# One shared pool of buffers, a throw-away tile for row sums, a plan that follows its ranks, and layer 1's diagonal addition on GpSimd

## The chip, the cores and the metric

The kernel runs on one core of a Trainium2 chip. A core has a matrix engine (TensorE, PE in the profile; its weight loads are shown apart as PEld), a vector engine (VectorE, DVE), a scalar engine (ScalarE, ACT), a general engine (GpSimd, POOL) and SyncE (SP), whose queue only issues transfers here. Each engine works through its own instructions in program order, and waits at a semaphore where an instruction needs something that isn't there yet. All matrices are 32-bit floats. The metric is the device time of one launch in microseconds (us); less is better.

## What is computed

Sixteen independent graphs ("batches") of N = 1024 nodes with 128 features each, and a 1024 x 1024 matrix `adj` for each, pass four layers. Each layer starts with a layer norm and a ReLU and ends with an addition to x:

```python
# layer 0, three times over, h the normed input (no relu after the third)
h = h @ W + b
nh = h / max(norm(h), EPS);  cos = nh @ nh.T
h = relu((adj * cos) @ h)
# layer 1 (y is 0 where nodemask is off)
y = relu(((1 + eps) * h + adj.T @ h) @ W1 + b1) @ W2 + b2
# layer 2
h = h @ W;  attn = softmax(where(adj > 0, tanh(s1[:, None] + s2[None, :]), -1e15))
y = where(rows without a neighbour, input, attn @ h)
# layer 3
h = x @ W.T + b;  e = h A h.T + its transpose
att = softmax(where(adj > 0, e, 0), axis=1) * adj
hp = relu(att @ h)          # then three sigmoid gates over [x, hp]
```

## The kernel before

**Tiles.** A node block is 128 nodes, so a graph has 8 blocks (`NB`), and a 1024 x 1024 matrix is 8 pieces of 128 x 1024. Products are made in halves of 512 columns, one PSUM bank each. `adj` is read twice: transposed (`adjT`, function `turn`, for layers 0, 2 and 3), and as it stands (`adjL`, function `layer1`). For `adjT` the transfer puts squares of 32 x 32 in place (L1518) and DVE turns each square (L1526). For batch 0 the pieces come as they are (`raw`, L1494) and PE turns them.

**Layer 0 and layer 3** need a symmetric product (`Square`, from L1341). `row(j, s)` makes only the blocks on and over the diagonal on PE (L1363). The blocks under it are mirrored: PE transposes them (L1373) from copies that `keep` made in the tile `above` of 22 blocks, or, in the batches 1 to 13, the lower left quarter goes through HBM: DVE transposes 32 x 32 squares into `above` (L1385), SP's queue stores them (L1412) and fetches them into `got` (L1422). DVE then multiplies each half with `adjT` (L1598 in layer 0, L1863 and L1904 in layer 3), and PE adds the products up (L1431, L1442).

**Row sums.** Layer 2 needs to know which rows have no neighbour. ACT copies each piece of `adjT` onto itself and keeps the sum of each row in `su` (L1529), so all who use `adjT` come after that copy.

**Layer 1.** For each of the 8 pieces `adjL` a transfer is issued (L1476, `load_adj`); then DVE adds (1 + eps) on the diagonal of the piece, one 128 x 128 block (`ident_e`, L1643); then PE multiplies (L1431). 

**GpSimd's work**: the inverse square roots of the layer norms (`rstd`) and of layer 0's norms (`rn`), both at L1165; one product of layer 3's end (`z`, L2008); four products in the last two batches (L1900); and at the start the transfers of the parameters (L278).

**The order of the work.** Nothing is issued as it is written down. Every operation becomes an `Op` with an engine, a cost in us, what it reads and writes, and a rank: a due time from the table `TIMES` plus the batch number times `PERIOD` (L1070). `Plan.order` (L135) then builds one list; each engine's program is its part of that list. It keeps a clock for each engine. At each step it looks at all operations whose predecessors are in the list, works out the earliest time at which each could start (its engine is free, its inputs are there, its buffer is free), takes the engine with the earliest of those, and on it, among the operations that can start within `WINDOW` = 0.05 us of that time, the one of lowest rank. An operation of a batch more than `AHEAD` = 2 past the oldest unfinished one isn't taken, transfers excepted. Operations marked `port` (those of DVE that read two tiles of SBUF, and some others) and all of GpSimd's share one more clock in the plan, `port`, so that the plan never lays one over the other:

```python
if o.port and port > at:
    at = port
```

**Buffers.** A `Buf` takes a slot in a pool when its first writer is placed, and gives it back after its last user. `POOLS` says how many slots each pool has, `KINDS` which pool a kind uses, how many of it there may be in all, and how many by batches other than the oldest. Before the change there are separate pools: 16 slots for `adjT`, 5 for `adjL` and `raw`, 3 for x, 13 (`big`) for all other tiles of 128 x 1024 and a little more (`w4`, `chunk`), and 2 for `above`.

Of the kernel before, what the change touches and what calls it, by code (L numbers as in the profile page):

```python
# [34 lines left out]
class Buf:  # L35


    def __init__(self, kind, shape, name):
        self.kind, self.shape, self.name = kind, shape, name
        self.slot = self.t = None  # L40
        self.uses = 0
        self.seen, self.users = [], []
        self.end = 0.0
# [12 lines left out]
class Plan:  # L56
# [78 lines left out]
    def order(self):  # L135
# [12 lines left out]
        rows = {e: i for i, e in enumerate(self.LATENCY)}  # L148
        while ready:
# [4 lines left out]
            found = []  # L154
            for o in ready:
                if o.batch > oldest + self.ahead and o.engine != "DMA":
                    continue
                at = max(free[o.engine], o.from_)
                if o.port and port > at:
                    at = port  # L160
                if o.new:
                    need, room = {}, {}
                    for b in o.new:
                        need[b.kind] = need.get(b.kind, 0) + 1
                    for k, n in need.items():
                        pool, most, share = self.kinds[k]
                        if total[k] + n > most or (o.batch > oldest and young[k] + n > share):
                            at = None
                            break
                        room[pool] = room.get(pool, 0) + n  # L170
                    if at is not None:
                        for pool, n in room.items():
                            if len(state[pool]) < n:
                                at = None
                                break
                            at = max(at, state[pool][n - 1][0])
                    if at is None:
                        continue
                found.append((at, o))
            if not found:  # L180
                stuck = [b.name for o in ready if o.batch == oldest for b in o.new]
                raise RuntimeError(f"no slot for any of {stuck}")
            first = min(found, key=lambda f: (f[0], rows[f[1].engine]))
            at, o = min(
                (f for f in found if f[1].engine == first[1].engine and f[0] <= first[0] + self.window),
                key=lambda f: f[1].rank,
            )
# [34 lines left out]
def tile_adj_preln(  # L222
# [40 lines left out]
    FLAGS = set("CabcdkxhyzTGmrHWMD3n")  # L263
# [4 lines left out]
    nc.vector.memset(half, 0.5)  # L268
    mhalf = const.tile([P, NB], F32, name="mhalf")
# [55 lines left out]
    for load_it in first:  # L325
# [11 lines left out]
    POOLS = {"adjT": 16, "adjL": 5, "x": 3, "big": 13, "above": 2, "got": 1, "bank": 8, "small": 29, "row": 6, "hbm": 3, "hrow": 2, "mask": 5, "dot": 12}  # L337
    KINDS = {
        "adjT": ("adjT", 16, 16), "adjL": ("adjL", 5, 5), "x": ("x", 3, 3), "w4": ("big", 9, 5),
        "chunk": ("big", 10, 12), "above": ("above", 2, 1), "got": ("got", 1, 1), "ps": ("bank", 7, 8),  # L340
        "acc": ("bank", 7, 8), "small": ("small", 7, 16), "row": ("row", 3, 3), "hbm": ("hbm", 3, 3),
        "hrow": ("hrow", 1, 1), "mask": ("mask", 5, 5), "dot": ("dot", 6, 11),
    }
    PERIOD, AHEAD, WINDOW = 145.06, 2, 0.05

    TIMES = {
        "T DMA raw <0": [51.6, -92.65, -42.9, 3.5, 39.85, 7.55, 4, 14.6],
        "T PE raw <0": [8.95, 14, 0.9, 0.1, 1.8, 11.5, 24.3, 8.7, 10.25, 24.85, 23.15, 30.8, 27.8, 31.75,
            37.1, 39.05],
        "T ACT adjT <0": [10.4, 39.05, 8.5, 13.4, 18.8, 14.95, 18.55, 20.55, 23.6, 34, 35.15, 28.45, 39.25,  # L350
            43.8, 44.95, 62.3],
        "T DVE su <0": [53.8],
        "x DMA x <0": [51.55, -93.7],
        "0 DVE st <0": [3.5, 4.1],
        "0 DVE mv <0": [9.55],
        "0 POOL rstd <0": [4.05],
        "0 DVE nb <0": [8],
        "0 DVE hn <0": [9],
        "0 ACT hn <0": [38.8],
        "0 PE ps <0": [0.3, 12.55],  # L360
        "0 ACT hT <0": [-29.95, 13.25],
        "00 PE psP <0": [-4, -11.9],
        "00 DVE h <0": [12.3, 13.05],
        "00 PE ps <0": [23.7, 4.25],
        "00 ACT hTn <0": [15.5, 15.95],
        "00 ACT sq <0": [9.5, 16.45],
        "00 DVE ss <0": [-0.4, 17.4, 18.1],
        "00 POOL rn <0": [31.75],
        "00 PE sq <0": [5.9, 23.6, 7.2, 24.25, 13.15, 8.2, 10.5, -25.2, 6.35, 35.5, 21.75, 22.95, 30.8,
            27.05, 27.75, 40.9, 34.6, 52.3, 47.45, 25.15, 52.8, 47.65],  # L370
        "00 ACT above <0": [16.8, 25.9, 20.15, 21.45, 21.05, 27.1, 27, 35.15, 44.25, 39.55],
        "00 DVE ew <0": [20.55, 22.4, 22.5, 36.85, 24.55, 30.55, 38.4, 34.95, 29.5, 42.65, 33.2, 41.35, 48.7,
            51.6, 44.75, 54.3],
        "00 PE acc0 <0": [1.15, 16.5, 13, 10.35, 16.8, 17.8, 23.5, 23.4, 29.8, 44.65, 39.75, 41, 36.25,
            62.05, 45.45, 57.85],
        "00 POOL params <0": [36.5, 32.1, 45.3, 53, 56.95, 59.45, 57.95],
        "00 DMA params <0": [51.15],
        "00 DVE params <0": [65.55, 68.05, 68.05, 72.5, 77.85],
        "00 PE params <0": [46.25, 59.4, 67.2],
        "00 ACT hT <0": [71.35, 58.35],  # L380
        "01 PE psP <0": [48.7, 58.7],
        "01 DVE h <0": [69.85, 69.8],
        "01 PE ps <0": [62.15, 55.8],
        "01 ACT hTn <0": [74.6, 77.8],
        "01 ACT sq <0": [88.4, 75.85],
        "01 DVE ss <0": [76.35, 76, 75.35],
        "01 POOL rn <0": [85.7],
        "01 PE sq <0": [69.35, 77.1, 67.35, 71.05, 69.5, 61.9, 71.9, 72.55, 83.05, 79.35, 79.85, 82.25,
            81.65, 86.95, 89.5, 88.15, 86.6, 87.9, 88.85, 85.6, 88.85, 80.2],
        "01 ACT above <0": [84.55, 78.6, 81.55, 80.85, 88.55, 86.7, 99.05, 90.1, 98.25, 100.1],  # L390
        "01 DVE ew <0": [78.05, 92.3, 81.45, 86.7, 87.75, 96.2, 92.9, 91.6, 93.85, 100.95, 89.4, 98.6, 96.4,
            111.05, 92.4, 91.6],
        "01 PE acc0 <0": [73.8, 85.1, 79.95, 79.7, 80.75, 79.35, 85.55, 82.95, 86.65, 87, 85.75, 88.7, 88.55,
            92.6, 90.25, 95.7],
        "01 ACT hT <0": [102.35, 105.3],
        "02 PE psP <0": [93.5, 94.1],
        "02 DVE h <0": [111.55, 105.55],
        "02 PE ps <0": [95.75, 93.15],
        "02 ACT hTn <0": [114.45, 109.95],
        "02 ACT sq <0": [139.5, 103.55],  # L400
        "02 DVE ss <0": [110.85, 118.05, 110.75],
        "02 POOL rn <0": [132.95],
        "02 PE sq <0": [104.2, 101.25, 108.75, 111.1, 102.75, 106.15, 102.05, 93, 108.8, 109.9, 109.8, 115.1,
            115.55, 112.1, 119.5, 119.95, 122.9, 111.5, 118.6, 122.3, 121.85, 129.35],
        "02 ACT above <0": [114.75, 122.65, 108.55, 121.65, 119, 120.9, 125.85, 129.8, 136.8, 145.15],
        "02 DVE ew <0": [113.15, 105.5, 117.9, 112.35, 125.6, 119.95, 118.75, 124.8, 129.8, 126.4, 126.55,
            132.7, 131.6, 126.8, 122.9, 141.5],
        "02 PE acc0 <0": [115.6, 116.45, 107.95, 105, 109.15, 114.05, 117.4, 112.55, 132.75, 118.2, 123.05,
            131.2, 113.55, 121.5, 124.25, 117],
        "02 DVE x <0": [137.5, 138.95],  # L410
        "T DMA adjT <1": [-127.65, -137.2, -158.65, -112.3, -198.45, -149.5, -107.65, -98.7],
        "T DVE adjT <1": [-118.5, -112.1, -110.7, -105.6, -102, -90.25, -86.2, -85.25],
        "T ACT adjT <1": [-112.4, -112.9, -110.15, -106.5, -87.15, -73.4, -90.65, -89.55],
        "1 DVE st <0": [135.85, 142.2],
        "1 DVE mv <0": [141.85],
        "1 POOL rstd <0": [135.1],
        "1 DVE nb <0": [144.4],
        "1 DVE hn <0": [140.7],
        "1 ACT hn <0": [139.15, 139.6],
        "1 DVE x <0": [143.2, 166.35, 170],  # L420
        "1 DMA adjL <0": [51.6, 65.9, 63.85, 62.15, 49.9, 160.9, 153.9, 153.25],
        "1 DVE adjL <0": [80.75, 72.65, 82.35, 76.45, 78.15, 151.65, 156.4, 161.25],
        "1 PE acc1 <0": [135.6, 136.4, 137.3, 138.1, 140.45, 138.5, 143.45, 140.85, 143.9, 142.2, 148.6,
            147.5, 149.25, 146.5, 153.05, 144.3],
# [1712 lines left out]
```

## Time and profile before

The three runs took 2382.04, 2385.14 and 2384.33 us, median 2384.33. The profiled execution took 2384.38 us, of which the span from its first to its last instruction is 2382.6 us.

| engine | busy us | share of the span | instructions |
|---|---|---|---|
| PE (matmul) | 2346.0 | 98% | 11577 |
| PEld (weight load) | 1552.4 | 65% | 11577 |
| DVE | 2038.7 | 86% | 5570 |
| ACT | 1435.5 | 60% | 2561 |
| POOL | 247.7 | 10% | 168 |

The rows of the profile give an instruction's line, engine and operation, "out<-in" by the program's tile names, how often it ran, and after the bar the busy time, the mean time of one in ns, and the idle time of its engine just before it with what ended that. The chain of work that ended last is followed back from the last instruction to whatever released each step. A 32-bit matmul of the program is two instructions on PE, a transpose is one. Starts and ends of matmuls overlap[...].

### The profile page before, as it was taken

The page shows a single profiled execution, that of the slowest core. Times are in us where ns is not written, and L with a number is a line of the kernel's source. Part 1 is how long each engine was busy: PE and PEld are TensorE (multiplying, and loading weights), DVE is VectorE, ACT ScalarE, POOL GpSimd, SP SyncE. Part 2 cuts the span into 40 slices and gives each one's busy share as a digit, 9 for nine tenths or more (in the row PEclk, how much of TensorE's full clock was granted, in tenths as well). Part 3 has the DMA queues.
Part 4 walks back from the last instruction along what each step waited for, and adds up shares of the span by engine and source line. Part 5 has one row for each costly group of instructions (what it writes and reads, how often), then busy time and mean ns, then how long its engine had stood idle before and what let it go on. Part 6 is the DMA issues. An engine that isn't in the chain of part 4 may idle for free.

```text
span 2382.6 us, 35138 instructions
## 1 busy us (share of the span) xinstructions
PE 2346.0 (98%) x11577; PEld 1552.4 (65%) x11577; DVE 2038.7 (86%) x5570; ACT 1435.5 (60%) x2561; POOL 247.7 (10%) x168
## 2 busy tenths in 40 slices
PE   8999999999999999999999999999999999999997
PEld 5568566675757657566675766757576575765764
DVE  6658798998988989899898989989899898887676
ACT  7325765756566565765756567465765756655375
POOL 3001010100101101010100101001011100100012
PEclk9999999999999999999999999999999999999999
DMA  9332938668585875949769496775948768165000
GB/s 195 88 107 63 177 92 185 149 135 167 123 177 138 148 168 130 178 109 183 156 125 183 108 181 142 146 168 132 164 129 164 160 128 158 49 112 115 19 10 18
DMA packets 997254, 314.31 MB, mean 132 GB/s; under 512 B 682456, under 2 KB 978528, under 8 KB 997072
## 3 DMA queue, kind: packets, MB, share of 16 engines
q1 hardware_dynamic: 976912, 301.35, 61.0%
q10 hardware_dynamic: 19264, 9.70, 1.4%
q8 instruction: 92, 1.51, 0.3%
q0 software_dynamic: 896, 1.01, 0.2%
q14 instruction: 90, 0.74, 0.1%
HBM read 227.50 MB, written 84.47 MB: 131 GB/s over the span
## 4 chain that ended last, share of the span: by engine, by line
PE 95%; ACT 2%; DVE 1%; SPq 1%; DMA 1%; issue 0%; POOL 0%; DVEq 0%; ACTq 0%; POOLq 0%
PE acc L1431 36%; PE sq L1363 20%; PE acc L1442 19%; PE psP L1203 6%; PE sq L1373 4%; PE py L1660 2%; PE py L1213 2%; PE psN L1203 1%; PE pg L1213 1%; PE ps_hTn L1172 1%; SPq L1518 1%; PE ps_hnT L1172 1%; PE ps_h3T L1172 1%; DMA raw<-in_adj_dram 0%; ACT hT L1225 0%
## 5 line engine op out<-in xcount | busy, mean ns | idle before, releaser
L1598 DVE SCALAR_TENSOR_TENSOR ew<-sq,rn,adjT 128x512 f32<-128x512 f32 x612 | 439.2, 739 | 58.7 <-PE sq L1373 25.4
L1431 PE MATMUL acc<-ew,h 128*128 128x512 f32 x1024 | 484.4, 595 | 4.3 <-DVE ew L1598 4.3
L1363 PE MATMUL sq<-hTn 128*128 128x512 f32 (+3 forms) x1152 | 438.1, 489 | 0.8 <-ACT hTn L1225 0.5
L1398 ACT COPY above<-sq 128x384 f32<-128x384 f32 (+3 forms) x432 | 167.6, 392 | 353.7 <-PE sq L1373 260.5
L1363 PEld LDWEIGHTS sq<-hTn 128*128 128x128 f32 x1152 | 195.0, 191 | 144.7 <-issue 104.6
L1431 PEld LDWEIGHTS acc<-ew,h 128*128 128x128 f32 x1024 | 181.1, 191 | 162.3 <-issue 122.2
L1442 PEld LDWEIGHTS acc<-h,ew 128*128 128x128 f32 x2048 | 246.1, 192 | 35.6 <-issue 30.1
L1442 PE MATMUL acc<-h,ew 128*128 128x128 f32 x2048 | 252.8, 275 | 0.5 <-DVE ew L1598 0.5
L1442 PEld LDWEIGHTS acc<-h,e 128*128 128x128 f32 x2048 | 236.8, 192 | 22.6 <-issue 16.7
L1431 PE MATMUL acc<-e,hs 128*128 128x512 f32 x512 | 241.9, 593 | 4.4 <-ACT hs L1913 4.3
L1442 PE MATMUL acc<-h,e 128*128 128x129 f32 x2048 | 238.4, 275 | 1.9 <-DVE e L1772 1.9
L1165 POOL TENSOR_TENSOR rstd<-ve,mhalf 128x8 f32<-128x8 f32 x64 | 106.2, 1660 | 1228.4 <-DVE ve L1284 1228.3
L1431 PE MATMUL acc<-adjL,hn 128*128 128x512 f32 x512 | 232.7, 592 | 0.0
L1863 DVE CUSTOM_DVE_ANT_0 e<-mask,sq 128x512 f32<-128x512 int8 x204 | 136.2, 676 | 65.2 <-ACT above L1398 58.1
L1904 DVE TENSOR_TENSOR e<-e,adjT 128x512 f32<-128x512 f32 x248 | 162.7, 678 | 30.2 <-ACT e L1895 30.0
L1373 PEld LDWEIGHTS sq<-ident,above 128*128 128x128 f32 x960 | 124.4, 142 | 88.6 <-issue 71.2
L1529 ACT ACTIVATE adjT<-adjT 128x1024 f32<-128x1024 f32 x120 | 126.5, 1055 | 85.9 <-DVE adjT L1526 85.3
L1373 PE MATMUL sq<-ident,above 128*128 128x128 f32 x960 | 174.5, 274 | 0.0
L1385 DVE STREAM_TRANSPOSE above<-sq 128x512 f32<-128x512 f32 x208 | 146.0, 703 | 28.7 <-PE sq L1363 28.5
L1772 DVE SCALAR_TENSOR_TENSOR e<-adjT,e 128x512 f32<-128x512 f32 x256 | 163.0, 689 | 4.3 <-ACT e L1768 4.3
L1431 PEld LDWEIGHTS acc<-adjL,hn 128*128 128x128 f32 x512 | 93.6, 190 | 98.1 <-issue 86.2
L1431 PEld LDWEIGHTS acc<-e,hs 128*128 128x128 f32 x512 | 92.4, 190 | 98.5 <-issue 75.0
(164 smaller groups left out, 3645.7 us busy)
## 6 DMA issues: line engine op xcount, KB each, us to landing
adjL<-in_adj_dram SPq DMA_DIRECT2D x128, 512.0 KB
adjT<-in_adj_dram SPq DMA_DIRECT2D x480, 128.0 KB
by_hbm<-above SPq DMA_DIRECT2D x104, 512.0 KB
got<-by_hbm SPq DMA_DIRECT2D x416, 128.0 KB
s<-sd SPq DMA_DIRECT2D x15, 512.0 KB
out_dram<-z ACTq DMA_DIRECT2D x15, 512.0 KB
d_hT<-hn SPq DMA_DIRECT2D x14, 512.0 KB
hT<-d_hT SPq DMA_DIRECT2D x56, 128.0 KB
```

The source lines that it names most:

```text
L1203: nc.tensor.matmul(dst.t[:, (c - lo) * n : (c - lo + 1) * n], cols(srcT.t, c), w, start=True, stop=True)
L1363: lambda: nc.tensor.matmul(dst.t[:, (first - lo) * P :], cols(leftT.t, j), span(rightT.t, first, hi), start=True, stop=True),
L1373: nc.tensor.transpose(cols(dst.t, r), cols(above.t, p), ident)
L1385: lambda: nc.vector.transpose(self.apart(j // 2).rearrange("p (h r q i) -> p r h q i", r=2, q=QUARTER, i=SQ)[:, j % 2], read.t.rearrange(" ...
L1398: lambda: nc.scalar.copy(span(above.t, p, p + hi - first), read.t[:, (first - lo) * P :]),
L1431: lambda s=s, lo=lo, hi=hi: nc.tensor.matmul(acc[s].t, cols(h.t, at, w), span(ew.t, lo, hi), start=(j == 0), stop=(j == NB - 1)),
L1442: nc.tensor.matmul(a.t[:, (c - lo) * n : (c - lo + 1) * n], cols(ew.t, c), h.t[:, at * w : at * w + n], start=(j == 0 and c == lo), stop=( ...
L1529: lambda t=t, c=c: nc.scalar.activation(t.t, t.t, AF.Copy, accum_out=su.t[:, c : c + 1]),
L1598: lambda view=view, ew=ew, rn=rn, j=j, lo=lo, hi=hi: nc.vector.scalar_tensor_tensor(like(view(), span(ew.t, lo, hi)), view(), rn.t[:, j : ...
L1772: lambda e=e, j=j, lo=lo, hi=hi: nc.vector.scalar_tensor_tensor(span(e.t, lo, hi), span(aT[j].t, lo, hi), 0.0, span(e.t, lo, hi), op0=ALU. ...
L1863: lambda e=e, view=view, mask=mask, peak=peak, s=s, lo=lo, hi=hi: nc.vector.tensor_tensor_reduce(like(view(), span(e.t, lo, hi)), like(vie ...
L1904: lambda e=e, j=j, lo=lo, hi=hi: nc.vector.tensor_mul(span(e.t, lo, hi), span(e.t, lo, hi), span(aT[j].t, lo, hi)),
```

## The change

- **Pools.** `adjT`, `adjL`, x, `w4` and `chunk` now share one pool, `big`, of 40 slots. The tile `above` is split: `near` (6 blocks, the pool `near` with 2 slots) and two `quart` tiles of 8 blocks each, which are slots of `big`. The limits in `KINDS` are new. The number of products on PE, and how the lower quarter is made, stay as they were.
- **Row sums.** ACT no longer copies `adjT` onto itself. It writes to one tile of bytes, `unused`, which nobody reads, and the operation writes only `su`.
- **The plan.** `order` takes, among the operations that are ready and whose buffers fit, the one of lowest rank, whatever the clocks say. The clock of the shared port is gone for the operations (`dve` and `pool_op` no longer pass `port`); GpSimd's costs are raised by 8% in the plan instead. All of `TIMES` is new, and `PERIOD` goes from 145.06 to 144.24.
- **Layer 1.** With the new flag `U` GpSimd adds the diagonal.

```diff
-    FLAGS = set("CabcdkxhyzTGmrHWMD3n")
+    FLAGS = set("CabcdkxhyzTGmrHWMD3nU")
+    unused = const.tile([P, N], I8, name="unused")
-    POOLS = {"adjT": 16, "adjL": 5, "x": 3, "big": 13, "above": 2, "got": 1, "bank": 8, "small": 29, "row": 6, "hbm": 3, "hrow": 2, "mask": 5, "dot": 12}
+    POOLS = {"big": 40, "near": 2, "got": 1, "bank": 8, "small": 29, "row": 6, "hbm": 3, "hrow": 2, "mask": 5, "dot": 12}
     KINDS = {
...
+        "adjT": ("big", 17, 24), "adjL": ("big", 5, 4), "x": ("big", 9, 4), "w4": ("big", 14, 23),
+        "chunk": ("big", 9, 9), "near": ("near", 2, 2), "quart": ("big", 8, 12), "got": ("got", 1, 1),
+        "ps": ("bank", 7, 6), "acc": ("bank", 7, 4), "small": ("small", 9, 21), "row": ("row", 5, 2),
...
-    PERIOD, AHEAD, WINDOW = 145.06, 2, 0.05
+    PERIOD, AHEAD, WINDOW = 144.24, 2, 0.05
```

```diff
-            first = min(found, key=lambda f: (f[0], rows[f[1].engine]))
-            at, o = min(
-                (f for f in found if f[1].engine == first[1].engine and f[0] <= first[0] + self.window),
-                key=lambda f: f[1].rank,
-            )
+            o = next((o for o in sorted(ready, key=lambda o: (o.rank, o.seq)) if fits(o)), None)
...
     def dve(us, reads, writes, fn, port=False):
-        return op("DVE", us + 0.015, reads, writes, fn, port)
+        return op("DVE", us + 0.015, reads, writes, fn)
     def pool_op(us, reads, writes, fn):
-        return op("POOL", us, reads, writes, fn, True)
+        return op("POOL", us * 1.08, reads, writes, fn)
```

```diff
             act(
-                S(N, False, True), [t], [t, su],
-                lambda t=t, c=c: nc.scalar.activation(t.t, t.t, AF.Copy, accum_out=su.t[:, c : c + 1]),
+                S(N, False, True), [t], [su],
+                lambda t=t, c=c: nc.scalar.activation(unused, t.t, AF.Copy, accum_out=su.t[:, c : c + 1]),
             )
...
-            self.above = Buf("above", [P, 22 * P], f"above_{k}")
+            self.near = Buf("near", [P, 6 * P], f"near_{k}")
+            self.quart = [Buf("quart", [P, N], f"quart_{k}_{i}") for i in range(2)]
...
-            o = dve(
-                STT, [blk(a_in, j, j + 1)], [blk(a_in, j, j + 1)],
-                lambda j=j, a_in=a_in: nc.vector.tensor_add(cols(a_in.t, j), cols(a_in.t, j), ident_e), True,
-            )
+            if "U" in FLAGS:
+                o = pool_op(
+                    0.45, [blk(a_in, j, j + 1)], [blk(a_in, j, j + 1)],
+                    lambda j=j, a_in=a_in: nc.gpsimd.tensor_add(cols(a_in.t, j), cols(a_in.t, j), ident_e),
+                )
```

The rest of the diff adds code behind flags that are not set (a second way of turning tiles through HBM, another end of layer 3), and the names that the split of `above` needs.

## The prediction

> **What bounds the kernel.** I read the busy shares, then the chain, then a stretch of the middle, and last the two ends.
>
> ```profile
> PE 2346.0 (98%) x11577; PEld 1552.4 (65%) x11577; DVE 2038.7 (86%) x5570; ACT 1435.5 (60%) x2561; POOL 247.7 (10%) x168
> PE 95%; ACT 2%; DVE 1%; SPq 1%; DMA 1%; issue 0%; POOL 0%; DVEq 0%; ACTq 0%; POOLq 0%
> 543.42 8.58 PE acc L1431 x20
> 470.86 10.05 PE acc L1442 x90
> 101.86 0.87 PE sq L1373 x8
> 543.42:830.99 287.57, 287.07 (x1408) 189.18 (x1407) 258.76 (x703) 178.69 (x314) 26.72 (x17) 1.00 0.73 151
> ```
>
> Line 1 is busy time, line 2 the engines' shares of the chain; then three pieces of the chain in order of time (start, length, what, how many); the last is one stretch (length, then busy PE, PEld, DVE, ACT, POOL, granted clock, DMA share). PE holds 95% of the chain. But is a PE that is busy for 98% at its limit? **A rule against the row:** the Trainium skill (Perfetto Trace Analysis, Identifying the Most-Contended Engine) says that matmul busy time is a bad measure, since matmuls are pipelined, and wants the weight loads' share. By it, 65%, a third of the time could be won by feeding PE better. The chain pieces have a finer measure, the time from start to start: 8.58/20 = 0.429 us for 512 columns, 10.05/90 = 0.112 for 128, 0.87/8 = 0.109 for a transpose. In the trace 384 columns take 0.323 and 256 take 0.216. With the counts of the groups: 3008 x 0.429 + 256 x 0.323 + 256 x 0.216 + 6440 x 0.112 + 1617 x 0.109 = 2326 us. The span is then
>
> lead to the first matmul 7.7 + matmuls at their own rate 2325.7 + stalls 38.4 + tail after the last 10.7 = 2382.5 us.
>
> So 57 us at the very most can be won while PE's work stays as it is, not a third. I take the row. The stalls (gaps from start to start over a form's usual one, summed in the trace) lie at 11.0 us before 100 us, 14.5 in 100 to 2250, 12.9 after. Two batches of the middle take 287.57 us, the same to 0.02 in the next two, with 1.2 us of stalls: 0.4%. DVE is busy for 90% there.
>
> The largest stall:
>
> ```profile
> 61.20 0.17 DVE L1687 TENSOR_SCALAR alone<-su 128x8 f32<-128x8 f32 x1 [1.22 <-ACT adjT L1529]
> 68.22 2.08 DVE L1598 SCALAR_TENSOR_TENSOR ew<-got,rn,adjT 128x512 f32<-128x512 f32 x3 [6.85 <-DMA adjL<-in_adj_dram]
> PEld acc L1431 <- DVE ew L1598: 4.2, 1, 4.2
> 50.00:100.00 50.00, 45.98 (x174) 26.00 (x173) 34.59 (x90) 15.63 (x31) 4.87 (x3) 0.93 0.47 120
> ```
>
> DVE's queue stands still for 6.85 us (61.4 to 68.2) at an operation that reads `got`, the quarter of batch 1's square that comes back from HBM: the plan put it there too early, behind transfers that were still running. PE starves for 4.2 us, and its next matmuls start 0.8 to 1.0 us apart instead of 0.43: the granted clock in this stretch is 0.93. All 7.3 us of stalls between 50 and 100 us are this place.
>
> **The change part by part.** *PE's work*: the products and their number stay: 0.
>
> *Row sums*: ACT's operation has the same input, accumulator and number (120). Writing bytes costs ACT nothing new: the masks written as bytes take 1050 ns for 1024 columns, the copy 1055. Users of `adjT` no longer come after ACT; no row shows PE waiting for that, so 0 on the path.
>
> *Layer 1's diagonal*:
>
> ```profile
> L1643 DVE TENSOR_TENSOR adjL<-adjL,ident_e 128x128 f32<-128x128 f32 x128 | 35.1, 283 | 5.5 <-DMA adjL<-in_adj_dram 5.3 <-issue 0.2
> L1165 POOL TENSOR_TENSOR rstd<-ve,mhalf 128x8 f32<-128x8 f32 x64 | 106.2, 1660 | 1228.4 <-DVE ve L1284 1228.3
> L1984 POOL TENSOR_TENSOR z<-z,x 128x1024 f32<-128x1024 f32 x1 | 2.4, 2352 | 0.1
> ```
>
> DVE loses 128 x 0.283 = 35.1 us (after the bar: busy us, mean ns, idle before) and four waits of 5.3 us in all. Both lie beside PE: 0 on the path in the middle. On GpSimd the price is unknown: at least 2.352/8 = 0.29 us by columns from its own addition; at most the 1.64 of its smallest operations, which are powers. I take 0.44, the addition's 0.29 plus the fixed 0.15 that DVE's own rows show (0.283 for 128 columns, 0.678 for 512). That is 56 us more (37 to 210), POOL 304 us of 2383: far from a bound. The wait moves with it: an addition whose piece hasn't landed now holds up GpSimd's queue, and behind it stand `rstd`, `rn` and `z`; for `rn` DVE's products wait, for those PE. The waits were at most 2.3 us each on DVE; at those sizes the lead of two batches hides them. No DMA issue moves with the addition, though the new order moves all transfers on SP's queue.
>
> *The port.* **The second rule speaks against the change.** The plan kept GpSimd and DVE apart; now it doesn't. The skill (SBUF — State Buffer, Who interferes with whom) says that a GpSimd operation and a DVE operation with two SBUF inputs, or in a two-port mode, exclude each other for a whole instruction. The trace agrees where the old plan missed it:
>
> ```profile
> 2292.72 2.36 POOL L1900 TENSOR_TENSOR e<-e,adjT 128x1024 f32<-128x1024 f32 x1 [7.07 <-ACT e L1895]
> 2292.95 2.22 DVE L1706 TENSOR_SCALAR hrow<-hsum 128x128 f32<-128x128 f32 x1
> 2295.22 0.49 PE L1713 MATMUL pf<-w2f,hrow 128*128 128x128 f32 x2 [1.15 <-DVE hrow L1706]
> 2305.31 4.68 DVE L1772 SCALAR_TENSOR_TENSOR e<-adjT,e 128x512 f32<-128x512 f32 x4 [0.23 <-ACT e L1768]
> ```
>
> L1706 takes 2.22 us instead of 0.278, one of the L1772 takes 2.87 instead of 0.68, and PE waits 1.15 us for the first. L1598 on a product in PSUM isn't touched (743 ns under a GpSimd operation, 740 without). By the rule's worst, each GpSimd operation costs DVE its full length: (26.72 + 16 x 0.44) = 33.8 us per two batches, and DVE would need 258.8 - 4.5 + 33.8 = 288 us, more than PE's 286.4: nothing won, some 6 us lost over the middle. By the rows, operations of this kind (L1772, L1904, those on `got`, L1247 and L1990 on SBUF, L1842: 653 us) are a third of DVE's time; a power of 1.64 us spans two or three DVE operations, so about half will hit one and cost it about 1 us; with the rest that is about 80 us in all, 10 per two batches: DVE 264 of 287, 92%. I take the rows: PE covers it in the middle, and 2 us are lost at the end, where DVE is on the chain.
>
> *Pool and order.* 37 slots in four pools become 40 in one, of which each square takes two. Transfers can start earlier; DVE's waits for `adjT` were 7.0 us in all. How the new order falls can't be read from the old trace; its worth is bounded by the stalls: 0 to -38 us, or a gain turned into new stalls, which have no bound above. Nearest rows: the stall at 61 to 74 us is one misplaced `got` and has no cause in the amount of work; a different order will hardly repeat it, but the start is when transfers are slowest (DMA share 1.02 over the first 50 us), so I count -5 of 7.3. The middle has 1.2 per two batches, half at a short wait for `hT`: -2 of 14.5. The end is the last batch's own chain through layers 2 and 3: -3 of 12.9. Lead and tail: the same first transfer and last gates, 0.
>
> Sum: -5 - 2 - 3 + 2 = -8, so 2384.4 - 8 = 2376 for the profiled execution (span 2382.6 and 1.8 around it), which stands at the median of 2384.3: **2376 us**.
>
> **The rivals.**
> 1. *Much of the slack goes* (both ends well ordered). For: 24 of the 38 us lie in the outer 235 us. Against: the last batch's chain has nothing left to overlap. 12 from the start and end, 8 from the middle: 2364.
> 2. *Nothing to win*: PE's rate hides all, and new stalls of 38 us take the place of the old. For: 99.6% in the middle. 2384.
> 3. *Slower: the port reaches PE.* Each GpSimd operation that catches a DVE operation which PE is about to need costs PE 1.1 to 1.7 us, as at 2295 and 2307 us. The place is layers 2 and 3 of each batch (L1772, L1904), with other batches' `rstd`, `rn` and additions falling into them. Five or six such hits eat the 8 us; from the sixth on it decides. At 13 in the middle, one a batch: 2376 + 20 = 2396. Against: nearly a batch of lead, and DVE idle for 28 us of 287.
>
> **How the numbers follow.** Likeliest case 0.47 (own range 2369 to 2382), rival 1 0.16, rival 2 0.15, rival 3 0.22. The measurement tells about 0.2%, 4.8 us, from no change. Of the likeliest case 0.43 is under 2379.5, with rival 1 0.59; same 0.18 (rival 2 and the rest, some of rival 3's mild end counted against it); slower 0.23. The range leaves out a tenth at each end: 2362 to 2395.
>
> **What would show it.** Right: two batches at 286.4 to 287.5 us with DVE at about 264; no 6.85 us wait before 100 us; L1643's successor on POOL at 0.3 to 0.5 us; stalls of about 30 us in all. L1772 and L1904 with a mean above 0.70 us show the port; where PE's waits name them in the middle, rival 3 holds. Two batches well under 286 us would prove my count of PE's work wrong.

## The result, and the profile after

The changed kernel takes **2375.07 us** (median of 6, 2372.78 to 2377.41), the kernel before 2383.18 in the same comparison (6 runs, 2380.45 to 2385.85). The ratio is 0.9966, 95% interval 0.9954 to 0.9979: faster by 0.34%. The forecast was 2376. The profiled execution took 2377.41 us, the slowest of the six, with a span of 2375.6.

The page's busy shares and the engines' shares of the chain, after:

```profile
PE 2342.0 (99%) x11577; PEld 1552.5 (65%) x11577; DVE 2023.8 (85%) x5442; ACT 1452.0 (61%) x2561; POOL 313.6 (13%) x296
PE 94%; DVE 4%; ACT 1%; DMA 1%; issue 0%; SPq 0%; POOL 0%; DVEq 0%; ACTq 0%; POOLq 0%
```

PE has the same 11577 instructions. DVE has 128 fewer, POOL 128 more. In the chain PE, ACT and SP's queue hold a point less each, and DVE holds 4% instead of 1%.

The span by the sum of the prediction (starts to starts, as before), both profiled executions in us:

| | lead | matmuls at their own rate | stalls before 100 us | middle | last 132.6 us | tail | span |
|---|---|---|---|---|---|---|---|
| before | 7.7 | 2325.7 | 11.0 | 14.5 | 12.9 | 10.7 | 2382.6 |
| after | 7.3 | 2325.7 | 5.8 | 7.8 | 18.2 | 10.7 | 2375.6 |
| difference | -0.4 | 0 | -5.2 | -6.7 | +5.3 | 0 | -7.0 |

Each row's items add up to the span within 0.1. So in this execution the kernel won 12 us at the start and in the middle, and gave 5 back at the end. It is one profile of each kernel, and the changed kernel's lies 2.3 us over its median.

**Start.** Windows of after (length, then busy PE, PEld, DVE, ACT, POOL, granted clock, DMA share, GB/s), then the timeline of the place with the large stall:

```profile
50.00:100.00 50.00, 48.88 (x199) 28.13 (x198) 33.79 (x69) 25.46 (x47) 3.74 (x3) 1.00 0.40 101
734.40:1020.60 286.20, 286.20 (x1408) 189.25 (x1407) 255.37 (x687) 180.95 (x315) 35.25 (x32) 1.00 0.71 151
1020.60:1306.90 286.30, 286.30 (x1408) 189.35 (x1408) 255.65 (x688) 180.94 (x316) 35.24 (x32) 1.00 0.73 151
```

```profile
61.56 4.03 PE L1478 MATMUL acc<-ew,h 128*128 128x512 f32 x9
65.89 2.08 DVE L1645 SCALAR_TENSOR_TENSOR ew<-got,rn,adjT 128x512 f32<-128x512 f32 x3 [5.17 <-DMA adjL<-in_adj_dram]
66.70 3.70 PE L1478 MATMUL acc<-ew,h 128*128 128x512 f32 x8 [1.12 <-DVE ew L1645]
```

DVE still stands for 5.17 us (60.72 to 65.89) at the operation on `got`. But PE has work until 65.58, of which line 1 shows the last nine matmuls, and waits 1.12 us instead of 4.0. The granted clock of these 50 us is 1.00 instead of 0.93; an estimate from these figures is that this alone is worth 50 x 0.07 = 3.5 us.

**Middle.** Two batches take 286.2 and 286.3 us instead of 287.57; DVE is busy for 255.4 and 255.7 of them. The stall that went is short and came once a batch. The timeline of before, at one of the twelve places, then the same step of after:

```profile
492.76 2.31 PE L1431 MATMUL acc<-ew,h 128*128 128x512 f32 x5
494.90 0.60 PE L1172 MATMUL ps_hTn<-ident,h 128*128 128x128 f32 x4
495.10 0.60 ACT L1225 ACTIVATE hT<-acc 128x512 f32<-128x512 f32 x1
495.75 1.49 PE L1203 MATMUL psP<-w,hT 128*128 128x128 f32 x11 [0.25 <-ACT hT L1225]
```

```profile
487.78 1.45 PE L1478 MATMUL acc<-ew,h 128*128 128x512 f32 x3
489.06 2.01 PE L1249 MATMUL psP<-w,hT 128*128 128x128 f32 x16
489.27 0.60 ACT L1271 ACTIVATE hT<-acc 128x512 f32<-128x512 f32 x1 [3.17 <-PE acc L1478]
```

ACT starts the eviction `hT` 0.04 us after the last product in both kernels. It takes 0.60 us, and before the change PE's program had only four transposes between that product and the matmuls which read `hT`: it cost PE 0.41 us each time, start to start. After, PE has products with the other half of `hT` to do meanwhile (part of the 16 in one row) and doesn't wait. Between 500 and 1900 us the stalls fell from 6.4 us to 0.3. That window, after:

```profile
500.00:1900.00 1400.00, 1400.00 (x6842) 922.84 (x6842) 1250.78 (x3356) 887.16 (x1538) 172.59 (x158) 1.00 0.72 152
```

PE has not one idle moment in 1400 us that the profile can see.

**GpSimd and the port.** Groups of after (after the bar: busy us, mean ns, idle before):

```profile
L1691 POOL TENSOR_TENSOR adjL<-adjL,ident_e 128x128 f32<-128x128 f32 x128 | 63.4, 512 | 92.5 <-DMA adjL<-in_adj_dram 73.6 <-PE acc L1478 12.1 <-DVE sum L1962 2.9
L1171 POOL TENSOR_TENSOR rstd<-ve,mhalf 128x8 f32<-128x8 f32 x64 | 108.8, 1699 | 812.4 <-DVE ve L1330 811.7
L1825 DVE SCALAR_TENSOR_TENSOR e<-adjT,e 128x512 f32<-128x512 f32 x256 | 162.1, 681 | 3.5 <-ACT e L1821 3.5
L1957 DVE TENSOR_TENSOR e<-e,adjT 128x512 f32<-128x512 f32 x248 | 168.6, 700 | 9.2 <-ACT e L1948 9.2
L2046 POOL TENSOR_TENSOR z<-z,x 128x1024 f32<-128x1024 f32 x1 | 2.7, 2672 | 0.1
```

The addition takes 455 ns (median) to 512 (mean). L1825 and L1957 are the L1772 and L1904 of before.

**End.** The timeline of after at three places of the last two batches:

```profile
2278.96 2.62 POOL L1953 TENSOR_TENSOR e<-e,adjT 128x1024 f32<-128x1024 f32 x1 [6.38 <-ACT e L1948]
2279.23 2.44 DVE L1759 TENSOR_SCALAR hrow<-hsum 128x128 f32<-128x128 f32 x1
2281.73 0.49 PE L1766 MATMUL pf<-w2f,hrow 128*128 128x128 f32 x2 [2.28 <-DVE hrow L1759]
...
2308.36 5.35 POOL L1953 TENSOR_TENSOR e<-e,adjT 128x1024 f32<-128x1024 f32 x2 [20.31 <-ACT e L1948]
2308.72 2.78 DVE L1957 TENSOR_TENSOR e<-e,adjT 128x512 f32<-128x512 f32 x1
...
2322.97 1.23 PE L1178 MATMUL ps_hnT<-ident,hn 128*128 128x128 f32 x6 [2.26 <-DVE hn L1347]
...
2344.51 2.67 POOL L2046 TENSOR_TENSOR z<-z,x 128x1024 f32<-128x1024 f32 x1
2345.50 2.23 DVE L1957 TENSOR_TENSOR e<-e,adjT 128x512 f32<-128x512 f32 x1
2348.50 0.40 ACT L1966 ACTIVATE hs<-h,sum 128x128 f32<-128x128 f32 x1 [3.43 <-DVE sum L1962]
...
2349.20 2.05 PE L1478 MATMUL acc<-e,hs 128*128 128x512 f32 x2 [2.55 <-ACT near L1450]
```

The collision of before has stayed (L1759, 2.44 us instead of 0.278; PE waits 2.28), and there are two more. At 2308 us L1957 takes 2.78 us instead of 0.68 under GpSimd's product; DVE is busy from there, but for 0.1 us, until the layer norm's `ve` at 2320, and PE waits 2.26 us for that norm's `hn`. At 2345 us L1957 takes 2.23 under `z`, ACT waits 3.43 us for a row sum behind it in DVE's program, and the eviction `near`, which is behind that on ACT, keeps PE waiting for 2.55.

### The profile page after: what moved, and what is told of

The parts are those of the page before. It is cut to its first block, busy times and chain, and to the rows that moved or that the text cites. A ratio compares the mean times of both kernels' runs of the same rounds, so it can differ in the third digit from the quotient of the medians.

```text
span 2375.6 us, 35092 instructions
## 1 busy us (share of the span) xinstructions
PE 2342.0 (99%) x11577; PEld 1552.5 (65%) x11577; DVE 2023.8 (85%) x5442; ACT 1452.0 (61%) x2561; POOL 313.6 (13%) x296
## 4 chain that ended last, share of the span: by engine, by line
PE 94%; DVE 4%; ACT 1%; DMA 1%; issue 0%; SPq 0%; POOL 0%; DVEq 0%; ACTq 0%; POOLq 0%
PE acc L1478 36%; PE sq L1415 20%; PE acc L1489 19%; PE psP L1249 6%; PE sq L1425 4%; PE py L1713 2%; PE py L1259 2%; PE ps_hTn L1178 1%; PE pg L1259 1%; PE psN L1249 1%; DVE e L1916 1%; PE ps_hnT L1178 1%; PE ps_h3T L1178 1%; DVE e L1957 0%; DVE e L1825 0%
## 5 line engine op out<-in xcount | busy, mean ns | idle before, releaser
L1645 DVE SCALAR_TENSOR_TENSOR ew<-sq,rn,adjT 128x512 f32<-128x512 f32 x612 | 431.7, 735 | 71.5 <-PE sq L1425 31.1
L1478 PE MATMUL acc<-ew,h 128*128 128x512 f32 x1024 | 476.6, 593 | 1.1 <-DVE ew L1645 1.1
L1415 PE MATMUL sq<-hTn 128*128 128x512 f32 (+3 forms) x1152 | 429.6, 487 | 0.0
L1450 ACT COPY near<-sq 128x128 f32<-128x128 f32 (+2 forms) x384 | 140.7, 370 | 353.5 <-PE sq L1425 276.5
L1948 ACT ACTIVATE e<-e,top 128x1024 f32<-128x1024 f32 x128 | 146.6, 1146 | 57.8 <-DVE top L1937 56.5
L1916 DVE CUSTOM_DVE_ANT_0 e<-mask,sq 128x512 f32<-128x512 int8 x204 | 135.5, 677 | 49.0 <-ACT near L1450 45.9
L1957 DVE TENSOR_TENSOR e<-e,adjT 128x512 f32<-128x512 f32 x248 | 168.6, 700 | 9.2 <-ACT e L1948 9.2
L1171 POOL TENSOR_TENSOR rn<-ss,mhalf 128x8 f32<-128x8 f32 x48 | 78.6, 1638 | 738.1 <-DVE ss L1632 622.1
L1825 DVE SCALAR_TENSOR_TENSOR e<-adjT,e 128x512 f32<-128x512 f32 x256 | 162.1, 681 | 3.5 <-ACT e L1821 3.5
L1425 PEld LDWEIGHTS sq<-ident,near 128*128 128x128 f32 x768 | 101.6, 141 | 83.8 <-issue 61.4
L1437 DVE STREAM_TRANSPOSE quart<-sq 128x512 f32<-128x512 f32 x208 | 144.2, 701 | 9.6 <-PE sq L1415 7.8
```

Of the source, the lines that this page charges most:

```text
L1171: pool_op(1.64, [src], [dst], lambda: nc.gpsimd.tensor_tensor(dst.t, src.t, mhalf, op=ALU.pow))
L1415: lambda: nc.tensor.matmul(dst.t[:, (first - lo) * P :], one(leftT, j), some(rightT, first, hi), start=True, stop=True),
L1425: nc.tensor.transpose(cols(dst.t, r), cols(kept.t, p), ident)
L1437: lambda: nc.vector.transpose(kept.t.rearrange("p (h r q i) -> p r h q i", r=2, q=QUARTER, i=SQ)[:, j % 2], read.t.rearrange("p (q h i) -> ...
L1478: lambda s=s, lo=lo, hi=hi: nc.tensor.matmul(acc[s].t, cols(h.t, at, w), span(ew.t, lo, hi), start=(j == 0), stop=(j == NB - 1)),
L1645: lambda view=view, ew=ew, rn=rn, j=j, lo=lo, hi=hi: nc.vector.scalar_tensor_tensor(like(view(), span(ew.t, lo, hi)), view(), rn.t[:, j : ...
```

## The experiments

Theory at the start: the time comes from PE's stalls and goes with the new order; GpSimd's addition and the throw-away tile are worth nothing by themselves. Rivals: the addition off DVE is what pays; the tile is; or the shared pool. All times are medians; the ratio is to the kernel before, measured beside each.

### The change without the addition on GpSimd

```diff
-    FLAGS = set("CabcdkxhyzTGmrHWMD3nU")
+    FLAGS = set("CabcdkxhyzTGmrHWMD3n")
...
-        "1 POOL adjL": [62.2, 69.05, 68, 67.15, 25.6, 37.8, 62.4, 79.95],
+        "1 DVE adjL": [62.2, 69.05, 68, 67.15, 25.6, 37.8, 62.4, 79.95],
```

(the same renaming in its four other rows; the programs of PE, ACT and SP stay as they are)

> The kernel after, with layer 1's diagonal addition back on DVE at the same due times; the order on PE, ACT and SP is the same row for row. Theory (the gain is the new order, the addition is hidden): 2373 to 2378 us, two batches of the middle at 286.2 to 286.6 with DVE at about 260 instead of 255.5. Rival (DVE's relief made the middle faster): two batches at 287.3 or more, 2381 us or more. Third view (the addition on GpSimd costs time through the port): 2372 or less.

Measured: 2375.90 us, ratio 0.9974 (0.9966 to 0.9983). Windows of this kernel:

```profile
734.40:1020.60 286.20, 286.20 (x1407) 189.34 (x1406) 257.84 (x703) 181.15 (x314) 27.34 (x16) 1.00 0.72 151
```

Not told apart from the changed kernel. DVE does 2.5 us more in two batches (257.84 against 255.37) and PE is full all the same: the moved addition was hidden on DVE too. What moves the time is in the rest of the change.

### The change with ACT's copies onto `adjT` again, planned

```diff
-                S(N, False, True), [t], [su],
-                lambda t=t, c=c: nc.scalar.activation(unused, t.t, AF.Copy, accum_out=su.t[:, c : c + 1]),
+                S(N, False, True), [t], [t, su],
+                lambda t=t, c=c: nc.scalar.activation(t.t, t.t, AF.Copy, accum_out=su.t[:, c : c + 1]),
```

(each copy due 1.3 us after DVE's turn of the same piece; only ACT's program changes its order)

> The kernel after, with ACT copying adjT onto itself again, each copy due 1.3 us after the turn on DVE; only ACT's program changes its order. Theory (the wait was never on PE's path): 2373 to 2379 us, the middle at 286.2 to 286.6. Rival (the junk tile made the gain by taking a wait from all users of adjT): 2381 us or more, and DVE's waits name ACT's copy with over 10 us.

Measured: 2408.86 us, 1.0110 (1.0097 to 1.0124), 34 us over the changed kernel. Waits of this kernel (us in all, times, longest):

```profile
PEld sq L1425 <- ACT near L1450: 41.3, 43, 3.4
PE sq L1425 <- ACT near L1450: 18.2, 25, 3.2
```

The copies, moved forward in ACT's program, stand ahead of evictions (`near`) that PE's transposes need. This mixes two things, the dependency and the place of the copies; a later run parts them.

### The kernel before with each edit alone, planned by the old rule

First the addition on GpSimd (its rows in `TIMES` renamed to match):

```diff
-            o = dve(
-                STT, [blk(a_in, j, j + 1)], [blk(a_in, j, j + 1)],
-                lambda j=j, a_in=a_in: nc.vector.tensor_add(cols(a_in.t, j), cols(a_in.t, j), ident_e), True,
+            o = pool_op(
+                0.455, [blk(a_in, j, j + 1)], [blk(a_in, j, j + 1)],
+                lambda j=j, a_in=a_in: nc.gpsimd.tensor_add(cols(a_in.t, j), cols(a_in.t, j), ident_e),
```

> The kernel before, with layer 1's diagonal addition on GpSimd and nothing else; its plan still keeps GpSimd and DVE apart, so parts of the order shift. Theory: 2379 to 2389 us, DVE's wait of about 6.9 us before 100 us is still there, two batches of the middle at about 287.5. Rival (the addition's move is the gain): 2378 or less, with the middle at 286.5.

Then the throw-away tile:

```diff
+    unused = const.tile([P, N], I8, name="unused")
...
-                S(N, False, True), [t], [t, su],
-                lambda t=t, c=c: nc.scalar.activation(t.t, t.t, AF.Copy, accum_out=su.t[:, c : c + 1]),
+                S(N, False, True), [t], [su],
+                lambda t=t, c=c: nc.scalar.activation(unused, t.t, AF.Copy, accum_out=su.t[:, c : c + 1]),
```

> The kernel before, with ACT writing the row sums' copies to a tile that nobody reads and nothing else. Theory: 2379 to 2389 us, the wait before 100 us and the 0.41 us stalls at hT stay. Rival (the removed wait is the gain): 2378 or less.

Measured: **2528.52 us**, 1.0607 (1.0592 to 1.0621), and **2562.64 us**, 1.0757 (1.0742 to 1.0771). Both expectations missed, by 139 us and more. PE's waits, of the first and of the second (its line numbers are one higher):

```profile
PE ps_hnT L1172 <- DVE hn L1301: 34.9, 10, 4.3
PE psP L1203 <- ACT hT L1225: 30.5, 21, 2.4
```

```profile
PE ps_hnT L1173 <- DVE hn L1302: 35.4, 10, 3.9
PE psP L1204 <- ACT hT L1226: 31.1, 22, 2.4
```

Two quite different edits give nearly the same new waits, at layer norms and evictions that neither touches. That points not at the edits but at the list: the old rule picks by earliest start, so a changed cost or dependency of one operation puts others elsewhere.

### The same two edits with the order held

The plan sees the old operation; only what is issued changes:

```diff
-                lambda j=j, a_in=a_in: nc.vector.tensor_add(cols(a_in.t, j), cols(a_in.t, j), ident_e), True,
+                lambda j=j, a_in=a_in: nc.gpsimd.tensor_add(cols(a_in.t, j), cols(a_in.t, j), ident_e), True,
```

> The kernel before with its whole order kept: only the diagonal additions are issued by GpSimd instead of DVE, at the places in the list that the old plan gave them. Theory (the addition's move is hidden, and what failed with the earlier try was the order that the old plan made of the changed costs): 2381 to 2387 us, two batches of the middle at 287.3 to 287.8, the wait of about 6.9 us before 100 us still there. Rival (GpSimd's additions themselves cost much outside the new plan): 2400 or more. Other rival (they are the gain): 2378 or less.

```diff
-                lambda t=t, c=c: nc.scalar.activation(t.t, t.t, AF.Copy, accum_out=su.t[:, c : c + 1]),
+                lambda t=t, c=c: nc.scalar.activation(unused, t.t, AF.Copy, accum_out=su.t[:, c : c + 1]),
```

> The kernel before with its whole order kept: only ACT's copies for the row sums go to a tile that nobody reads, so that the users of adjT need not wait for them. Theory: 2381 to 2386 us. Rival (the removed wait is worth something in itself): 2378 or less. If the tile alone does harm: 2390 or more.

Measured: **2382.71 us**, 0.9998 (0.9990 to 1.0006), and **2384.62 us**, 1.0001 (0.9992 to 1.0009). In the old order both edits are worth nothing, within 0.1%. The 145 and 180 us of the two runs before come only with the order that the plan makes of the edit.

### The change with the copies onto `adjT`, order held

The edit of the run with planned copies, but in what is issued alone; the plan stays that of the changed kernel.

> The kernel after with its whole order kept: only ACT's copies for the row sums go onto adjT again, so that later users wait for the copy and the copy waits for earlier users. If the 34 us of the earlier try came from where the copies were put in ACT's program, this costs little: 2374 to 2380 us. If the new order needs the tile because users are placed ahead of the copies or close behind them, DVE waits for ACT at L1645 and the time is 2385 or more.

Measured: 2393.53 us, 1.0043 (1.0030 to 1.0055), 18 us over the changed kernel. Waits of this kernel:

```profile
DVE ew L1645 <- ACT adjT L1576: 50.2, 24, 3.0
PE acc L1478 <- DVE ew L1645: 13.7, 12, 1.9
```

So the same tile is worth 0 in the old order and 18 us in the new one, which has layer 0's products closer behind the turn of their piece (L1645 is DVE's next instruction after 27 of the 120 turns; before the change L1598 was after 8). The other 15 us of the planned version come with the moved copies.

### Buffers apart again

The new ranks, with the slots of before for `adjT`, `adjL` and x (their limits in `KINDS` with them):

```diff
-    POOLS = {"big": 40, "near": 2, "got": 1, "bank": 8, "small": 29, "row": 6, "hbm": 3, "hrow": 2, "mask": 5, "dot": 12}
+    POOLS = {"adjT": 16, "adjL": 5, "x": 3, "big": 16, "near": 2, "got": 1, "bank": 8, "small": 29, "row": 6, "hbm": 3, "hrow": 2, "mask": 5, "dot": 12}
```

> The kernel after with slots of their own again for adjT (16), adjL and raw (5), x (3) and 16 for the rest, 40 in all; the ranks stay, and only 66 rows of PE's order and 156 of SP's move. Theory (the shared pool in itself is worth little; the ranks are what counts): 2373 to 2379 us with the middle at 286.2 to 286.8. Rival (sharing lets transfers start earlier and takes the stalls): 2381 or more.

Then only `adjT` apart, with the 17 slots that it may hold at most in the change, and the other 23 shared:

```diff
-    POOLS = {"big": 40, "near": 2, "got": 1, "bank": 8, "small": 29, "row": 6, "hbm": 3, "hrow": 2, "mask": 5, "dot": 12}
+    POOLS = {"adjT": 17, "big": 23, "near": 2, "got": 1, "bank": 8, "small": 29, "row": 6, "hbm": 3, "hrow": 2, "mask": 5, "dot": 12}
...
-        "adjT": ("big", 17, 24), "adjL": ("big", 5, 4), "x": ("big", 9, 4), "w4": ("big", 14, 23),
+        "adjT": ("adjT", 17, 24), "adjL": ("big", 5, 4), "x": ("big", 9, 4), "w4": ("big", 14, 23),
```

> The kernel after with 17 slots for adjT alone and 23 for everything else: the same limit of 17 that the new table sets for adjT anyway, and almost the same order on every engine (10 rows of PE's differ, none of SP's). If the trial with pools apart lost its 90 us because adjT had 16 slots where the new order wants 17: 2374 to 2382 us. If it lost them because a slot of its own pool is the one given back last, while a shared pool hands out the one that has been free for longest: 2395 or more, SP's queue waits for the last user of adjT (L1957) with over 200 us, and DVE's turn of adjT waits for transfers with over 50 us.

And with 16 (`"adjT": 16, "big": 24`):

> As the run with 17 slots for adjT, but with 16 for adjT and 24 for everything else; only adjT's count changes, adjL, x and the rest still share. If the 90 us of the pools apart came from the one slot of adjT that was missing: 2440 us or more, with DVE's turn of adjT (L1573) waiting for transfers with over 50 us. If they came from adjL and x having slots of their own: 2378 to 2390 us. In between, both have a part.

Measured: **2467.61 us** with all apart, 1.0353 (1.0339 to 1.0367); **2380.02** with 17 of its own, 0.9988 (0.9982 to 0.9995); **2453.46** with 16, 1.0295 (1.0279 to 1.0311). Waits with 16 of its own, then with 17:

```profile
SPq L1565 <- DVE e L1957: 353.8, 72, 26.9
...
DVE adjT L1573 <- DMA adjT<-in_adj_dram: 94.2, 26, 6.0
PE acc L1478 <- ACT hs L1966: 34.0, 11, 3.6
```

```profile
SPq L1565 <- DVE e L1957: 106.4, 27, 23.3
```

Two graphs hold 16 pieces. With 16 slots the transfer of a piece waits at the head of SP's queue until layer 3's last reader L1957 frees one, 354 us in all; the piece lands late, DVE's in-order program stands at the turn L1573 (94 us; 2.1 with 17), and behind it stands what PE needs: at 741 us, for one, the sum for `hs`, for which PE waits 3.4 us. The order hardly moved here: the traces show PE's and ACT's instructions in the run with 16 in the order of the changed kernel, row for row. One slot of `adjT` is worth 2453.5 - 2380.0 = 73 us; own slots for `adjL` and x too, 14 more; the sharing itself only 5 (2380.02 against 2375.07; the two intervals of the ratio don't overlap).

### More work on GpSimd

Behind each diagonal addition GpSimd adds two halves of the piece into a spare tile that nobody reads, so this kernel does more than is asked for; the programs of the other engines keep their order:

```diff
-                )
+                ); pool_op(1.2, [a_in], [], lambda a_in=a_in: nc.gpsimd.tensor_add(spare, span(a_in.t, 0, 4), span(a_in.t, 4, 8)))
```

> The kernel after with one more GpSimd operation behind each diagonal addition: it adds the halves of the same piece of adjL (128 x 512, two inputs in SBUF, about 1.2 us) into a tile that nobody reads; the order on the other engines is unchanged. It more than doubles GpSimd's time in the middle, and with it what can block DVE at the port. Theory (PE covers what DVE loses at the port in the middle): DVE 256 to 264 us per two batches, the middle at 286.2 to 287, 2374 to 2380 us. Rival 3 of the prediction (a blocked DVE operation reaches PE): over 1 us of PE stalls per batch, 2390 or more.

Measured: 2396.76 us, 1.0057 (1.0044 to 1.0070): the expectation that PE would cover it missed. One batch of this kernel's timeline:

```profile
830.84 1.27 POOL L1692 TENSOR_TENSOR spare<-adjL 128x512 f32<-128x512 f32 x1
831.04 3.32 DVE L1347 TENSOR_SCALAR hn<-x,mv,rstd 128x128 f32<-128x128 f32 x4
832.60 1.26 POOL L1692 TENSOR_TENSOR spare<-adjL 128x512 f32<-128x512 f32 x1
835.08 1.12 PE L1478 MATMUL acc<-adjL,hn 128*128 128x512 f32 x2 [1.00 <-ACT hn L1375]
```

Four L1347, each 0.34 us when nothing else runs, take 3.32 us here (one takes up to 1.45); ACT's ReLU of `hn` comes late, and layer 1's first matmul with it. PE waits 13.4 us for that in 14 places, once a batch; of the 21.7 us over the changed kernel the rest is not followed up. DVE was busy for 257 of 286 us there. So a DVE operation that GpSimd holds up can reach PE in the middle; the average share of DVE doesn't exclude it.

### The end on DVE

The plan of the changed kernel, but in the last two batches DVE does L1953's products and adds up `z`; `hp * gate` is folded into that:

```diff
-                pool_op(2.45, [e, aT[j]], [e], lambda e=e, j=j: nc.gpsimd.tensor_mul(e.t[:, 0:N], e.t[:, 0:N], aT[j].t))
+                pool_op(2.45, [e, aT[j]], [e], lambda e=e, j=j: nc.vector.tensor_mul(e.t[:, 0:N], e.t[:, 0:N], aT[j].t))
...
-                    pool_op(us, [blk(a, lo, hi, w), at], [blk(a, lo, hi, w)], lambda: nc.gpsimd.tensor_mul(part(a, w), part(a, w), per_node(of(g), n)))
-                    pool_op(us + 0.4 * n / NB, [blk(a, lo, hi, w), blk(c, lo, hi)], [blk(z, lo, hi)], lambda: nc.gpsimd.tensor_add(part(z), part(a, w), part(c)))
+                    pool_op(us, [blk(a, lo, hi, w), at], [blk(a, lo, hi, w)], lambda: None)
+                    pool_op(us + 0.4 * n / NB, [blk(a, lo, hi, w), blk(c, lo, hi)], [blk(z, lo, hi)], lambda: [nc.vector.scalar_tensor_tensor(cols(z.t, k), cols(a.t, k, w), gate.t[:, 3 * k + g : 3 * k + g + 1], cols(c.t, k), op0=ALU.mult, op1=ALU.add) for k in range(lo, hi)])
```

> The kernel after with GpSimd's large operations of the last two batches issued by DVE at the same places of the list: the four products of L1953, and the two gate steps of L2045 and L2046 as eight fused operations each. DVE gets some 10 us more work after 2250 us, and nothing large is left on GpSimd to block it there. Theory (the end lost 5 us to the port): L1759 at 0.28 instead of 2.44, stalls after 2250 us at 13 or less instead of 18, 2369 to 2373 us. Rival (DVE is full at the end, and its work costs as much there as the blocks did): 2374 to 2380.

Measured: **2371.46 us** (2370.12 to 2372.56), 0.9948 (0.9935 to 0.9962). This beats the kernel before by 0.5%. Against the changed kernel it is 3.6 us of medians: no run of the one lies in the range of the other (2372.78 is the lowest of the changed kernel), though the intervals of the two ratios overlap by 0.0008. The operations of `hrow` in this kernel, and its timeline near the end:

```profile
L1759 DVE TENSOR_SCALAR hrow<-hsum x16: 276/278/289, 179.8 to 2278.1; 128x128 f32<-128x128 f32 x16
```

```profile
2350.20 2.18 DVE L2046 SCALAR_TENSOR_TENSOR z<-z,gate,x 128x128 f32<-128x128 f32 x8
...
2353.81 1.98 PE L1478 MATMUL acc<-e,hs 128*128 128x512 f32 x4 [2.59 <-ACT hs L1966]
```

The longest L1759 of 16 is 289 ns; in the changed kernel it was 2445, and PE's stalls from 2276 to 2290 us (the same instructions in both) fall from 2.7 us to 1.2. (A product that GpSimd does in 2.6 us takes DVE 1.22.) The one at 2308 us is gone too: PE waits 0.60 us for that `hn` instead of 2.26. The last was only exchanged: PE no longer waits 2.55 us for `near`, but 2.59 for `hs`, because the additions of `z` now stand in DVE's own program. So gains of 1.5 us and 1.7 us are shown at two places. They can't be summed to the 3.6: the two profiles, of the slowest execution of the one kernel and the fastest of the other, lie 7.3 us apart, and the rest is spread over start and end in pieces of 1 to 2 us.

## Why the prediction was right, and where it was off

**Bound and sum.** Right. PE's floor is 2325.7 us in both, and two batches at 286.2 to 286.3 are 143.1 a batch with no gap. The measure from start to start held against the rule of the weight loads' share: that share is 65% in both kernels, while nothing but stalls could be won.

**The addition moved at no cost.** Right, shown twice: 0.9998 in the old order, and not told apart in the new one. Its price was 455 to 512 ns instead of my 440, so POOL is busy for 313.6 us instead of 304. It waits for pieces for 73.6 us in all (10.7 at most, where I had 2.3 from DVE's rows), and the run without it is no faster.

**The throw-away tile at 0.** Right for the order it was read from (1.0001), wrong as a statement on the change: the new order leans on it by 18 us. I asked whether PE waits for the copy in the old trace; I should have asked what a new order may put there once the dependency is gone.

**Start, -5.** Measured -5.2, but the sign I named for it was wrong in form. DVE's long wait did not go (5.17 us instead of 6.85). PE had work for 4.9 us when it began, instead of 3.6, and waited 1.12 us; behind that wait the granted clock stayed at 1.00, where it had fallen behind one of 4.0.

**Middle, -2.** The step that was mis-sized: it was -6.7. I had seen the short wait for `hT` as half of the middle's stalls and let it go only in part. It went altogether from 500 to 1900 us (6.4 to 0.3). That the new order did it is read from the two traces, by what PE has to do while `hT` is made; no run tried the new due times under the old rule, so rule and due times are not parted.

**End, -3 + 2 = -1.** Not so: +5.3 in the profiled execution, and +0.5 (13.4 us of stalls against 12.9) in the run without the flag, whose PE, ACT and SP have the same programs. The -3 did not come in either. One stretch of both, after first, then without the flag:

```profile
2320.00:2337.00 17.00, 14.59 (x64) 9.61 (x63) 8.95 (x27) 9.70 (x21) 7.59 (x4) 0.90 0.00 0
```

```profile
2320.00:2337.00 17.00, 15.54 (x80) 10.22 (x80) 10.48 (x38) 12.14 (x26) 8.04 (x4) 1.00 0.00 0
```

After, PE waits there for 2.26 us for the layer norm's `hn`, and twelve of the matmuls of 131 columns behind it start 0.22 us apart instead of 0.11; in the other run the wait is 0.94 us and they keep their pace. Behind the longer wait is the collision at 2308 us: in the run without the flag the same L1957 had started 0.43 us ahead of GpSimd's product and took 0.67 us. The longer wait is 1.3 us of the 5.3 and the slow clock behind it 1.7. The length of a wait alone doesn't decide the clock: after PE's 2.28 us at L1759 it stays at 1.00 (2281 to 2286 us), and in the run without the flag it falls to 0.76 after the same wait (2283 to 2290). The port's +2 at the end can't be checked as a term, since the kernel before had collisions there too (1.3 us of stalls at L1706, 1.7 at L1772); the changed kernel's at L1759 is 1.5 us by the run that removed it. The middle's -4.7 against my sum and the end's +6.3 nearly cancelled: that the total came out better than its parts is luck.

**The port, 10 us per two batches.** Much too large: it was 1.2, as DVE's 255.5 us stand against 258.8 - 4.5 = 254.3, and 0.6 in the first of the two windows if one adds up only what the operations that meet one of GpSimd's take over their usual time. The step that failed: "a power of 1.64 us spans two or three DVE operations, so about half will hit one and cost it about 1 us". In the new trace L1825 meets a power 32 times, in 22 of them starting under it, and takes 684 ns instead of 681: a power costs DVE nothing. It is the power that gets longer, about 2.0 us instead of 1.64 where L1825 started first. The rule of the Trainium skill (SBUF — State Buffer, Who interferes with whom), that whoever issues first blocks the other for the whole instruction, does not hold for a power that started first; the measurement decides.

For GpSimd's additions and products it does hold. L1957, which reads two tiles of SBUF, starts under one in 14 cases and ends 0.55 us after it in all of them; L1347 and L1759 end 0.08 to 0.09 us after it. L1645 on `sq`, a product in PSUM, keeps its time. So does one that starts 0.1 us or more ahead (L1957 682 and 684 ns at 2285 and 2308 us). So the loss is what is left of GpSimd's operation, and its length is the bound: with the addition's 0.455 us at most 0.2 us and 0.1 in the mean (L1347 448 ns instead of 340 in 41 meetings, L1957 775 instead of 681 in 13), with a 512-column addition of 1.26 us 0.9 in the mean (34 meetings of L1347 in the run with more work, 1260 ns), under a 1024-column operation up to 2.2. Over the whole kernel DVE lost about 20 us so, 12 of them in the last 133 us, where I had 80.

**Rival 3.** It did not decide; L1825 and L1957 stand at 681 and 700 ns, and PE's waits don't name them in the middle. Its mechanism is real with 512 columns on GpSimd, at another place than I gave it: the layer norm's `hn` while layer 1's pieces get their diagonal, about 1.3 us a batch (12.8 us of stalls from 500 to 1900 us, where the changed kernel has 0.3). A stage that makes a fresh input for PE was the place to look, not the stages with the most two-input work.

**Pools, "can't be read from the old trace".** True, but what the new order rests on is here: the 17th slot of `adjT` is worth 73 us to it, while the old order did with 16. The old trace showed DVE waiting only 7.0 us for `adjT`, from which I read that slots were worth little; that holds for the old order alone.

## What to carry to other kernels

Hold the order fixed when you ask what one edit is worth: with the list made anew, edits worth nothing cost 145 and 180 us, and a tile worth nothing in one order was worth 18 us in another. Count the slots of a buffer kind against what overlapping stages hold at once; the one beyond that can be worth more than all the arithmetic that is moved. Price a collision of GpSimd and DVE by what is left of GpSimd's addition or product when the DVE operation starts, and look for it where DVE makes what PE needs next: the three shown above lie in the last two batches.

## What the runs showed of the hardware that was not expected

- A GpSimd power on 128 x 8 lasts 1.64 us and leaves a DVE operation with two SBUF inputs untouched (684 ns under it, 681 without, 32 meetings). A GpSimd addition of 128 x 128 lasts 0.455 us and costs about 0.1, as the DVE operation ends only after it.
- L1347, a `tensor_scalar` with one tensor input, is held up by GpSimd's additions too (1260 ns instead of 341 under a 512-column one); the rule in the prediction allows that in a two-port mode, and no view shows the mode. L1916, a custom operation on a mask and a product in PSUM, is not (under an addition 674 ns, without 680).
- Some of GpSimd's own operations get longer under DVE: `rstd` up to 2.01 us instead of 1.64, the addition up to 0.98 instead of 0.455.
